# Seven steps of a window row, dealt out anew: where the residual, a centring and single taps stand in four in-order queues

## The chip, the cores and the metric

The kernel runs on one core of one Trainium2 chip. The metric is device time of one execution in microseconds (us). Engines: PE is TensorE (matrix products; PEld its weight loads), DVE is VectorE, ACT is ScalarE, POOL is GpSimd, SP issues the DMAs. Each engine takes its instructions in order, and the engines wait for one another by semaphores.

## The reference

Two layers on a batch of 16 images of 128 channels and 56 x 56 pixels, float32. The change touches the first alone, a block of attention over routed windows:

```python
x = x + dwconv3x3(x)                       # position
y = ln(x.transpose(0, 2, 3, 1), ln1)       # over channels
q, kv = split(y @ qkv_w + qkv_b)           # 7 x 7 windows of 8 x 8 pixels
idx = top_k(mean(q) . mean(k), 4)          # each window picks 4 windows
att = softmax(q_pix * SCALE @ k_sel)       # 4 heads, 64 queries x 256 keys
o = att @ v_sel + dwconv5x5(v)             # the second term is "lepe"
x = x + o @ wo_w + wo_b                    # residual
x = x + gelu(ln(x, ln2) @ w1 + b1) @ w2 + b2
```

The second layer (a 3 x 3 convolution, a small state space recurrence, a group norm) follows on the result.

## The kernel before, in words

The first layer works image by image, and each image in 49 steps, one for each window. Step t has row r = t // 7 and place c = t % 7 in the row. After the 49 steps `mlp` runs the two MLP products of seven row blocks and begins the next image. All instructions of an engine are chained in program order (`_chain`), so the order in which `step` calls its helpers is the order of every engine's queue.

What every step t does, and on which engine:

- `scores` (PE, L424) into the one buffer `ps`, then `largest` (VectorE, L430, the negated maximum), `exponentials` (ACT, L436, which reads `ps` and sums), `inverse` (VectorE, L442), `weights` (GpSimd, L446, two products).
- `attend` of window t - 2 (PE, L484), `transpose_weights` of window t - 1 (PE, L468, into `ptt`), `keep_weights` (ACT, L474).
- in even places `transpose_values` (PE, L454, into `pvt`) and `keep_values` (ACT, L461), for two windows, in c = 6 for one.
- `convolve_on`: taps of the 5 x 5 convolution on VectorE (L521 for a row's first, L527 for the others), 25 to a row, two rows in turns. `TAPS` says how many fall to each place; the last one comes at the step's end.
- `beside`: GpSimd's share of the next image's 3 x 3 convolution (L307, L323, L325), spread over all steps; `position` (L313) is that convolution's last tap, on VectorE, in six of the steps.

What a row adds, by place, for the finished row above (`out`, `row`) and for the same row of the next image (`nxt`):

- c = 0 and 1: products L364 for k and v of `nxt` into `g0` and their copies by ACT (`keep`, L370 and L373). c = 1: `collect` (VectorE, L531), `project_out` (PE, L539, into `pvt`).
- c = 2: `residual` (VectorE, L543) reads `pvt` and adds into `xh`; `centred` (PE, L329) multiplies `xh` by the centring matrix into `g0`.
- c = 3: `squared` (ACT, L333), `variance` (PE, L337, into `pvt`). c = 4: `deviation` (ACT, L341, L342), `second` (VectorE, L547: the norm's product, which reads `g0`), then `centred` for `nxt`, into `g0` again.
- c = 5 and 6: `squared`, `variance`, `deviation` for `nxt`; `windows` (VectorE, L350, L358); the product for q (L364).

`piece` issues PE's share of these. It stands ahead of `transpose_weights`, or, where `waits` holds (c = 1, 4, 6), at the end of the step. `surround` (GpSimd, L499 and two fills) copies a row of v with its neighbours into one of three buffers `vpad`, from which the taps read.

Of the kernel before, what the change touches and what calls it, by code (L numbers as in the profile page):

```python
# [209 lines left out]
def layer0(ctx: ExitStack, tc: tile.TileContext, x, t, x1, conv):  # L210
# [70 lines left out]
    def load(b, two):  # L281
        nc.sync.dma_start(pads[b % 2][64 * two : 64 * two + 64, 1 : H + 1, 1 : W + 1], xv[b, two])
# [48 lines left out]
    def squared(n):  # L331
        sq = held["sq"] = w1.tile([P, BLK], F32, tag="sq", name=f"sq_{n}")
        nc.scalar.activation(sq, held["pc"], AF.Square)  # L333
# [5 lines left out]
    def deviation(n):  # L339
        rstd = held["rstd"] = w1.tile([P, BLK], F32, tag="rstd", name=f"rstd_{n}")  # L340
        nc.scalar.activation(rstd, held["pv"], AF.Ln, bias=eps)  # L341
        nc.scalar.activation(rstd, rstd, AF.Exp, scale=-0.5)  # L342
# [3 lines left out]
    def windows(im, i):  # L346

        n = f"{im['b']}_{i}"
        y = held["y"] = w1.tile([P, BLK], F32, tag="y1", name=f"y1_{n}")
        nc.vector.tensor_mul(  # L350
            y.rearrange("c (w r x) -> c w r x", w=WIN, r=8),
            held["pc"].rearrange(by_row, r=8, w=WIN),
            held["rstd"].rearrange(by_row, r=8, w=WIN),
        )
        if i == 0:
            im["sum"] = w2.tile([P, NW], F32, tag="ysum", name=f"ysum_{n}")
            im["kv"] = w2.tile([P, NW, WP, 2], F32, tag="kv", name=f"kv_{n}")
        nc.vector.tensor_reduce(  # L358
            im["sum"][:, WIN * i : WIN * i + WIN], y.rearrange("c (w p) -> c w p", p=WP), AX.X, ALU.add
        )  # L360
# [5 lines left out]
    def keep(im, i, s):  # L366
        src = held["pq", s].rearrange("c (w p) -> c w p", p=WP)
        if s == 0:
            q = im["q"][i] = w1.tile([P, WIN, WP], F32, tag=f"q{i}", name=f"q_{im['b']}_{i}")
            nc.scalar.activation(q, src, AF.Identity, bias=bias[:, 0:1], scale=SCALE)  # L370
        else:
            kv = im["kv"][:, WIN * i : WIN * i + WIN, :, s - 1]
            nc.scalar.activation(kv, src, AF.Identity, bias=bias[:, s : s + 1])  # L373
# [27 lines left out]
    def gather(im, w):  # L401
        sel = im["sel", w] = w6.tile([P, TOPK, WP, 2], F32, tag="sel", name=f"sel_{im['b']}_{w}")
        if w % 2 == 0:
            n = min(2, NW - w)
            _, im["at"] = nc.values_load_multi_w_load_instructions(
                im["line"][:, w : w + n, :].rearrange("o w j -> o (w j)"), engines=(mybir.EngineType.SP,),
                min_val=0, max_val=NW - 1, skip_runtime_bounds_check_because="the indices are at most 48",
            )
        vs = im["at"][TOPK * (w % 2) :]
        for j in range(TOPK):  # L410
            nc.sync.dma_start(
                sel[:, j, :, :].rearrange("c p s -> c (p s)"),
                im["kv"][:, bass.ds(vs[j], 1), :, :].rearrange("c o p s -> c (o p s)"),
            )
# [76 lines left out]
    def vpad(im, r):  # L491
        return vpads[(im["b"] * NBLK + r) % 3]

    def surround(im, r):

        v = vpad(im, r)

        def put(lines, i, rows):
            nc.gpsimd.tensor_copy(  # L499
                v[:, lines, 2 : W + 2].rearrange("c r (w x) -> c w r x", x=8),  # L500
                im["kv"][:, WIN * i : WIN * i + WIN, :, 1].rearrange("c w (r x) -> c w r x", x=8)[:, :, rows, :],
            )

        put(slice(2, 10), r, slice(0, 8))
        if r == 0:
            nc.gpsimd.memset(v[:, 0:2, :], 0.0)
        else:
            put(slice(0, 2), r - 1, slice(6, 8))
        if r == NBLK - 1:
            nc.gpsimd.memset(v[:, 10:12, :], 0.0)  # L510
        else:
            put(slice(10, 12), r + 1, slice(0, 2))

    def convolve(im, r, k):

        v = vpad(im, r)
        acc = sums_[(im["b"] * NBLK + r) % 2][:, 0:BLK].rearrange("c (h w) -> c h w", w=W)
        dy, dx = divmod(k, 5)
        src = v[:, dy : dy + 8, dx : dx + W]
        if k == 0:  # L520
            nc.vector.tensor_scalar(acc, src, lep[:, 0:1], lepe_b, ALU.mult, ALU.add)  # L521
            return
        out = acc
        if k == 24:
            lepe = im["lepe", r] = w2.tile([P, BLK], F32, tag="lepe", name=f"lepe_{im['b']}_{r}")
            out = lepe.rearrange("c (h w) -> c h w", w=W)
        nc.vector.scalar_tensor_tensor(out, src, lep[:, k : k + 1], acc, ALU.mult, ALU.add)  # L527

    def collect(im, r):
        o = held["o"] = w1.tile([P, BLK], F32, tag="o", name=f"o_{im['b']}_{r}")  # L530
        nc.vector.tensor_add(  # L531
            o.rearrange("c (r w x) -> c r w x", r=8, w=WIN),
            po[:, 0:BLK].rearrange("c (w r x) -> c r w x", w=WIN, r=8),
            im["lepe", r].rearrange("c (r w x) -> c r w x", r=8, w=WIN),
        )
# [5 lines left out]
    def residual(im, r):  # L541
        xh = im["xh"][r]
        nc.vector.scalar_tensor_tensor(xh, held["pw"], wo_b, xh, ALU.add, ALU.add)  # L543

    def second(im, r):
        y2 = im["y2"][r] = w1.tile([P, BLK], F32, tag=f"y2{r}", name=f"y2_{im['b']}_{r}")
        nc.vector.tensor_mul(y2, held["pc"], held["rstd"])  # L547
# [19 lines left out]

    TAPS = (4, 2, 2, 3, 3, 3, 2)  # L570

    slot = [0]

    def convolve_on(count):


        for at in range(slot[0], slot[0] + count):
            r = at // 25
            r -= (r - at) % 2
            if 0 <= r < NB * NBLK:  # L580
                convolve(images[r // NBLK], r % NBLK, (at - 25 * r) // 2)
        slot[0] += count
# [14 lines left out]
    def open_step(im, t):  # L597
        scores(im, t)
        largest(im, t)

    def step(im, nxt, t):
        r, c = divmod(t, WIN)
        b = im["b"]
        n = f"{b}_{t}"
        out, row = (im, r - 1) if r else (images[b - 1], NBLK - 1)
        old, new = r > 0 or b > 0, nxt is not None
        if t + AHEAD < NW:
            gather(im, t + AHEAD)
        if t == 0 and early and not new:
            conv.load(0)  # L610
        if t in (20, 24) and b + 2 < NB:
            load(b + 2, t // 4 - 5)

        if c < 3 and new and r:
            keep(nxt, r - 1, c)
        if c == 2 and old:
            residual(out, row)
        if c == 3 and old:
            squared(n)
        if c == 4 and old:  # L620
            deviation(n)
        if c == 5 and new:
            squared(n)
        if c == 6 and new:
            deviation(n)
        if t > 0 or b == 0:
            open_step(im, t)
        if t > 1:
            attend(im, t - 2)
        if c == 1 and r:  # L630
            collect(im, r - 1)
        if c == 4 and old:
            second(out, row)
        if c == 6 and new:
            windows(nxt, r)
        convolve_on(TAPS[c] - 1)
        if new:
            ends, lead = (ENDS[1], LEAD) if b else (ENDS[0], FIRST)
            if t in ends:
                position(nxt, 1 + ends.index(t), (8,))  # L640
            if t < 45:
                beside_to(b + 1, lead + -(-(ROUND - lead) * (t + 1) // 45))
            else:
                beside_to(b + 2, 3 * (t - 44) // 2)
        exponentials(im, t)
        inverse(im, t)
        if t in (1, 8, 17, 27):
            surround(im, 3 + (1, 8, 17, 27).index(t))
        if t in (36, 44) and new:
            surround(nxt, (t - 36) // 8)  # L650
        weights(im, t)
        if c == 1 and new and r:
            project(g0, 2)
        waits = c in (1, 4, 6)
        if not waits:
            piece(im, nxt, out, row, c, r)
        if t > 0:
            transpose_weights(im, t - 1)
            keep_weights(im, t - 1)
        if c % 2 == 0:  # L660
            transpose_values(im, t)
            keep_values(im, t)
        convolve_on(1)
        if waits:
            piece(im, nxt, out, row, c, r)
# [85 lines left out]
    im = images[0]  # L751
# [63 lines left out]
    route(im)  # L815
    for w in range(AHEAD):
        gather(im, w)
    convolve_on(13)
    conv.bring()
    if NB > 1:  # L820
        beside_to(1, FIRST)
# [1 line left out]
    for b in range(NB):  # L823
        im, nxt = images[b], images[b + 1] if b + 1 < NB else None
# [5 lines left out]
    r = NBLK - 1  # L830
# [571 lines left out]
```

## Time and profile before

| | us |
|---|---|
| median of 3 runs | 8286.96 (8285.49 to 8291.58) |
| the profiled execution, its own time | 8287.32 |
| its span, first to last instruction | 8285.5 |
| first maximum of image 1, of image 2 | 285.9, 474.8 |
| last store's addition of the first layer ends | 3146.1 |
| first exponential of the second layer | 3187.7 |

So the first layer takes some 189 us an image. The granted TensorE clock is 0.985 of full speed over the span. In the profile a line names engine, source line, operation, the tile written and the tiles read; `sst` are the statistics of a step, `e` its exponentials, `g` is `g0`.

### The profile page before, as it was taken

Reading aid. Unit: us, or ns where it says so; the run is one execution under the profiler, and the core shown is the slowest. Engines: PE = TensorE matmul, PEld = TensorE weight load, DVE = VectorE, ACT = ScalarE, POOL = GpSimd, SP = SyncE. Lnnn points to the kernel's source line nnn. Section 1 sums busy time; section 2 is a strip of 40 time slices with the busy share of each in tenths; the row PEclk is TensorE's granted clock in tenths of the full one; section 3 lists DMA queues with packets and bytes.
Section 4 is the critical chain, followed back from the end, with each engine's and each line's share of the span. In section 5 each row is a group of like instructions: output and inputs, shape, how many; then the busy total and the mean of one; then the engine's idle time right before and its main releaser. Section 6 shows DMA issues by size and latency. Waiting matters only on the chain.

```text
span 8285.5 us, 151813 instructions
## 1 busy us (share of the span) xinstructions
PE 7838.8 (95%) x53380; PEld 3344.5 (40%) x53380; DVE 7607.8 (92%) x10105; ACT 5689.0 (69%) x10695; POOL 7010.1 (85%) x5569
## 2 busy tenths in 40 slices
PE   8999999999999998999999999999999999999998
PEld 4444444444444453333333333333333333333333
DVE  7998999999999976999999999999999999999998
ACT  5777777777777765666666666766666666666665
POOL 6888888888888725898989989999989989989897
PEclk9999999999999998999999999999999999999998
DMA  4333333333333223334333333334334344334333
GB/s 78 88 86 79 88 88 87 88 86 89 91 87 87 73 81 82 86 93 104 101 90 99 98 93 102 95 94 107 84 102 105 86 103 103 89 96 108 88 91 87
DMA packets 765510, 757.89 MB, mean 91 GB/s; under 512 B 189648, under 2 KB 664912, under 8 KB 762832
## 3 DMA queue, kind: packets, MB, share of 16 engines
q1 hardware_dynamic: 764752, 748.19, 35.4%
q8 instruction: 426, 6.98, 0.4%
q14 instruction: 332, 2.72, 0.1%
HBM read 439.61 MB, written 102.76 MB: 65 GB/s over the span
## 4 chain that ended last, share of the span: by engine, by line
PE 42%; DVE 28%; POOL 12%; ACT 10%; issue 7%; DMA 0%; SPq 0%; POOLq 0%; ACTq 0%; DVEq 0%
PE pq L185 9%; PE a L1028 9%; DVE h L1046 6%; DVE a L1056 5%; POOL xh L325 5%; PE pq L1074 4%; DVE lepe L527 4%; DVE h L1061 4%; PE x L1039 4%; POOL tap L323 3%; POOL e L446 3%; PE pq L1108 3%; DVE sst L430 2%; ACT e L436 2%; ACT a L1031 2%
## 5 line engine op out<-in xcount | busy, mean ns | idle before, releaser
L1065 POOL TENSOR_TENSOR cst<-h,cb 128x1792 f32<-128x1792 f32 x784 | 3129.1, 3998 | 337.4 <-DVE h L1061 278.1
L1031 ACT ACTIVATE a<-a 128x896 f32<-128x896 f32 x1568 | 1415.8, 903 | 1185.7 <-PE x L1039 962.8
L1046 DVE TENSOR_TENSOR h<-x,bb 128x896 f32<-128x896 f32 x1568 | 1695.6, 1081 | 131.1 <-PE x L1039 98.9
L527 DVE SCALAR_TENSOR_TENSOR lepe<-vpad,lep,lepe 128x448 f32<-128x448 f32 x2688 | 1716.8, 677 | 0.5
L1028 PE MATMUL a<-dt,adec 32*128 32x448 f32 x6272 | 1616.6, 591 | 55.7 <-DVE h L1061 53.9
L1039 PE MATMUL x<-dtx,amask 32*128 32x448 f32 x6272 | 1620.5, 593 | 40.2 <-DVE h L1046 31.1
L1056 DVE TENSOR_TENSOR a<-a,h 128x896 f32<-128x896 f32 x1344 | 1464.8, 1090 | 68.9 <-ACT a L1031 65.7
L1061 DVE TENSOR_TENSOR h<-a,h 128x896 f32<-128x896 f32 x1344 | 1465.1, 1090 | 42.0
L446 POOL TENSOR_SCALAR e<-e,sst,zero 128x256 f32<-128x256 f32 x1568 | 855.0, 555 | 573.5 <-DVE sst L442 514.2
L436 ACT ACTIVATE e<-ps,sst 128x256 f32<-128x256 f32 x1568 | 726.9, 468 | 538.1 <-DVE sst L430 493.1
L1028 PEld LDWEIGHTS a<-dt,adec 32*128 32x128 f32 x6272 | 472.6, 184 | 1060.1 <-issue 298.7
L325 POOL TENSOR_TENSOR xh<-xh,tap 128x448 f32<-128x448 f32 x742 | 849.7, 1145 | 32.9
L185 PE MATMUL pq<-pad,conv 128*128 128x448 f32 x1890 | 834.7, 559 | 0.0
L1074 PE MATMUL pq<-cst,sel 128*32 128x448 f32 x6272 | 729.9, 550 | 0.0
L430 DVE TENSOR_REDUCE sst<-ps 128x2 f32<-128x512 f32 x784 | 539.8, 688 | 111.1 <-PE ps L424 83.1
L146 ACT ACT_TABLE_LOAD x484 | 621.0, 1283 | 9.3 <-PEq L1393 0.7
L1039 PEld LDWEIGHTS x<-dtx,amask 32*128 32x128 f32 x6272 | 473.5, 184 | 319.0 <-DVE h L1046 295.2
L468 PE MATMUL ptt<-ident,e 128*128 128x128 f32 x3136 | 521.9, 281 | 71.0 <-POOL e L446 61.6
L424 PE MATMUL ps<-sel,q 32*64 32x256 f32 x6272 | 541.7, 414 | 48.3 <-ACT e L436 35.8
L468 PEld LDWEIGHTS ptt<-ident,e 128*128 128x128 f32 x3136 | 371.2, 142 | 371.3 <-issue 184.4
L474 ACT COPY att<-ptt 128x512 f32<-128x512 f32 x784 | 457.8, 584 | 62.7 <-PE ptt L468 52.9
L185 PEld LDWEIGHTS pq<-pad,conv 128*128 128x128 f32 x1890 | 324.2, 189 | 357.9 <-issue 350.2
(184 smaller groups left out, 12330.0 us busy)
## 6 DMA issues: line engine op xcount, KB each, us to landing
sel<-kv SPq DMA_DIRECT2D x3136, 64.0 KB
bb<-db SPq DMA_DIRECT2D x336, 448.0 KB
cb<-dc SPq DMA_DIRECT2D x336, 448.0 KB
x<-r SPq DMA_DIRECT2D x112, 224.0 KB
pad<-x SPq DMA_DIRECT2D x16, 1568.0 KB
db<-bs SPq DMA_DIRECT2D x112, 224.0 KB
dc<-cs SPq DMA_DIRECT2D x112, 224.0 KB
bb<-db SPq DMA_DIRECT2D x112, 224.0 KB
```

The costliest lines, as they stand in the source:

```text
L185: self.nc.tensor.matmul(bank[:, 0:BLK], lhsT=self.weights[:, k, :], rhs=self.pad[:, 8 * i + dy : 8 * i + dy + 8, dx : dx + W], start=(k == ...
L325: nc.gpsimd.tensor_add(im["xh"][i], im["xh"][i], held["tap"])
L446: nc.gpsimd.tensor_scalar(e, e, im["st", w][:, 2, p : p + 1], zero, ALU.mult, ALU.add)
L527: nc.vector.scalar_tensor_tensor(out, src, lep[:, k : k + 1], acc, ALU.mult, ALU.add)
L1028: nc.tensor.matmul(a[:, k, :], lhsT=adec[rows, l4, :], rhs=p["dt"][rows, h, :], start=True, stop=True)
L1031: nc.scalar.activation(p["a", l, jp], p["a", l, jp], AF.Exp)
L1039: nc.tensor.matmul(x[:, k, :], lhsT=mask[rows, l4, :], rhs=p["dtx"][rows, h, :], start=True, stop=True)
L1046: nc.vector.tensor_mul(p["h", l][:, own(jp), :], px["x"], weight)
L1056: nc.vector.tensor_mul(a, a, before)
L1061: nc.vector.tensor_add(h, p["a", l, jp], h)
L1065: nc.gpsimd.tensor_mul(c, p["h", l], p["gate", 1, l].unsqueeze(1).to_broadcast([P, 4, BLK]))
L1074: nc.tensor.matmul(py[32 * j : 32 * j + 32], lhsT=sel[:, l4, :], rhs=p["c", l][:, j, :], start=False, stop=(l % 4 == 3), skip_group_check= ...
```

## The change

- `residual` goes from ahead of `largest` to behind it (c = 2).
- `piece` of c = 2, which is `centred` of the finished row, goes behind both transposes, to the end of the step.
- One tap is taken out of the group and put between `windows` and `second`: in c = 4 it runs ahead of `second`.
- `TAPS` has one tap fewer in c = 0 and one more in c = 1. The sum, 19 to a row, is the same. Ahead of the first step 14 taps run instead of 13.
- GpSimd's copies move: in the image's own steps from t = 1, 8, 17, 27 to 3, 10, 17, 26, for the next image from 36 and 44 to 38 and 45.

```diff
-    TAPS = (4, 2, 2, 3, 3, 3, 2)
+    TAPS = (3, 3, 2, 3, 3, 3, 2)
...
         if c < 3 and new and r:
             keep(nxt, r - 1, c)
-        if c == 2 and old:
-            residual(out, row)
         if c == 3 and old:
             squared(n)
...
         if c == 1 and r:
             collect(im, r - 1)
+        if c == 2 and old:
+            residual(out, row)
+        if c == 6 and new:
+            windows(nxt, r)
+        convolve_on(1)
         if c == 4 and old:
             second(out, row)
-        if c == 6 and new:
-            windows(nxt, r)
-        convolve_on(TAPS[c] - 1)
+        convolve_on(TAPS[c] - 2)
...
-        if t in (1, 8, 17, 27):
-            surround(im, 3 + (1, 8, 17, 27).index(t))
-        if t in (36, 44) and new:
-            surround(nxt, (t - 36) // 8)
+        if t in (3, 10, 17, 26):
+            surround(im, 3 + (3, 10, 17, 26).index(t))
+        if t in (38, 45) and new:
+            surround(nxt, (t - 38) // 7)
...
-        waits = c in (1, 4, 6)
+        waits = c in (1, 2, 4, 6)
...
-    convolve_on(13)
+    convolve_on(14)
```

## The prediction

> **What bounds the kernel now.** The first layer ends near 3146 us (its last store's addition, L565, by the timeline); nothing behind it changes, so only its 784 steps count. Read first the page's engine line, then the busy times of the stretch 300 to 2900 us, which holds steps of the first layer alone (the numbers after the engines: clock, DMA share, GB/s).
>
> ```profile
> PE 7838.8 (95%) x53380; PEld 3344.5 (40%) x53380; DVE 7607.8 (92%) x10105; ACT 5689.0 (69%) x10695; POOL 7010.1 (85%) x5569
> ```
>
> ```profile
> 300.00:2900.00 2600.00, 2393.70 (x23241) 1275.11 (x23234) 2366.32 (x4513) 1900.05 (x5014) 2128.80 (x3080) 0.99 0.34 86
> ```
>
> In that stretch PE is busy 2394 and DVE 2366 of 2600 us: neither alone is the bound, and only the order of one row's seven steps tells which wait ends last. So next the timeline of VectorE in image 6, steps 21 to 26 (row 3; c is the step's place in the row). Columns: start, us, instruction, count, [idle before, releaser].
>
> ```profile
> 1303.26 0.68 DVE L543 SCALAR_TENSOR_TENSOR xh<-pvt,vec,xh 128x448 f32<-128x448 f32 x1
> 1303.97 0.69 DVE L430 TENSOR_REDUCE sst<-ps 128x2 f32<-128x512 f32 x1
> ...
> 1305.74 0.17 DVE L442 RECIPROCAL sst<-sst 128x2 f32<-128x2 f32 x1 [0.49 <-ACT e L436]
> ...
> 1306.80 0.69 DVE L430 TENSOR_REDUCE sst<-ps 128x2 f32<-128x512 f32 x1 [0.30 <-PE ps L424]
> ...
> 1309.45 0.69 DVE L430 TENSOR_REDUCE sst<-ps 128x2 f32<-128x512 f32 x1
> 1310.56 0.62 DVE L547 TENSOR_TENSOR y<-g,rstd 128x448 f32<-128x448 f32 x1 [0.42 <-ACT rstd L342]
> ```
>
> The maxima (L430) of c = 0 to 5 start at 1297.67, 1300.71, 1303.97, 1306.80, 1309.45 and 1313.00. VectorE stands still mainly at the two places that the change attacks: 0.49 before the reciprocal of c = 2 and 0.42 before the norm's product (L547) of c = 4. TensorE in the same steps:
>
> ```profile
> 1301.01 1.02 PE L364 MATMUL g<-y,wqkv 128*128 128x448 f32 x2 [0.28 <-ACT kv L373]
> ...
> 1303.15 0.68 PE L424 MATMUL ps<-sel,q 32*64 32x256 f32 x8
> ...
> 1305.42 0.64 PE L454 MATMUL pvt<-ident,sel 128*128 128x128 f32 x4
> 1305.98 0.68 PE L424 MATMUL ps<-sel,q 32*64 32x256 f32 x8
> ...
> 1311.23 1.02 PE L329 MATMUL g<-xh,centre 128*128 128x448 f32 x2 [0.31 <-DVE y L547]
> 1312.18 0.68 PE L424 MATMUL ps<-sel,q 32*64 32x256 f32 x8
> ```
>
> The scores (L424) end 0.13 to 0.14 before the next maximum in c = 2, 3, 4 and 5 (1303.83 to 1303.97 is the first): those maxima wait for TensorE, not for VectorE. And TensorE's queue is in order: whatever stands in front of the scores delays them. Last, step 1 of image 6 and its window (the first number behind the five engines is the granted clock):
>
> ```profile
> 1235.53 0.97 PE L468 MATMUL ptt<-ident,e 128*128 128x128 f32 x4 [1.98 <-POOL e L446]
> ```
>
> ```profile
> 1235.30:1238.40 3.10, 2.77 (x26) 1.18 (x30) 3.10 (x8) 1.50 (x5) 3.10 (x7) 0.84 0.29 85
> ```
>
> **Unit times,** start to start within a busy queue, from these rows: tap 0.595, maximum 0.60, collect 0.53, residual 0.60, norm's product 0.54, reciprocal 0.08; on PE scores 0.61 (0.68 to the end), attend 0.36, weights' transposes 0.44, values' transposes 0.57, a 448-wide product 0.85, or 0.95 where it had to wait (1311.23 to 1312.18). From a maximum's start its reciprocal can start after 1.79 (0.69, 0.04 to ACT, 1.02 for two exponentials, 0.04), the next scores after 1.80, the next maximum after 2.61: c = 5 already runs at this floor.
>
> **The residual behind the maximum, centring last in step 2.** Before, the residual (1303.26) began 0.03 after project_out ended and was done 0.03 before scores(2) allowed the maximum: it cost nothing. That maximum is reached from c = 0 by ACT and PE: exponentials, copies, keep of kv (ends 1300.96), L364 at 1301.01, transposes, project_out, scores(2) at 1303.15. None of these is touched, so largest(2) stays at 6.30 behind largest(0). After, the residual runs 0.60 to 1.28 behind largest(2). The values' transposes write pvt, whose product the residual is still reading (one buffer, L541-543), so they start after it; the row shows such a wait in L329 behind L547, which reuses g0. Then centring, then scores(3): 1.28 + 0.05 + 0.57 + 0.90 + 0.68 + 0.13 = 3.61 from maximum to maximum, against 2.83: +0.78 a row. The two uncertain links are the release (0.04 to 0.15 in rows like 1311.23 and the old residual) and the product (0.85 to 0.95): +0.72 to +0.93. VectorE saves its 0.49 before the reciprocal (residual and tap cover the 1.79) and pays more before the next maximum. Queued behind the waiting transposes are centring and scores(3), behind these the whole next step; no DMA is moved. Squared and variance now come without their 0.22 wait: c = 3 goes from 2.64 to its floor, -0.03.
>
> **The tap ahead of the norm's product (c = 4).** Before: rstd let L547 begin 1.11 behind the maximum. With variance earlier rstd is ready about 0.82 behind it, but the tap puts L547 at 0.60 + 0.595 = 1.19. Centring of the next image waits for it (it reuses g0), and scores(5) for that: 1.19 + 0.62 + 0.06 + 0.95 + 0.68 + 0.13 = 3.63 against 3.55: +0.08. VectorE's 0.42 moves behind the last tap. In step 46, where a position tap in c = 3 had hidden rstd's wait, the step was 3.16: +0.47 there.
>
> **Taps dealt anew.** One fewer in c = 0: VectorE's 3.03 falls to 2.5, but scores(1) end 2.70 behind largest(0) and the maximum comes at 2.83. That 0.20 is lost again in c = 1, because largest(2) is fixed at 6.30. Only where a position tap makes c = 1 bind (3.56, steps 15 and 36) is it kept: -0.29 and -0.17. The 14th tap ahead costs 0.6 once, and no more than that even if nothing hides it.
>
> **GpSimd's copies.** A surround is 0.65 + 2 x 0.31 at most (1.26 of groups L499, 1.04 overlapped). In c = 3 weights are needed only behind L547's centring, with some 0.4 to spare, and GpSimd idles 0.5 to 1.7 there: taken at 0 (if the cover goes, up to 0.17 in step 11). Freed steps 8, 27, 36, 44 gain nothing, as they run like their neighbours. In step 26 (3.67) position (L313, 1.30 against 0.68) waits for GpSimd's sum; c = 4's reciprocal, now 1.19 + 0.54 + 0.595 = 2.32 behind its maximum, stands 1.31 ahead of the next one instead of 0.66, and that sum runs behind its weights: -0.6, of which the surround ahead of weights(26) takes back 0.1: -0.5. In steps 0 to 2, weights(0) come a tap earlier, 1.98 of PE idle falls to about 1.4, and step 1 loses its surround. Images 1 to 14 take 11.13 there on average; image 10, at clock 1.0, took 9.52. By the sum above (3.70, 6.80, 10.4 in image 6) the mean is about 10.45: -0.7.
>
> The Trainium skill (TensorE: Matmul & The Clock Gate, What's actually happening) lets the clock halve after an idle window of about 3.4 us. The trace shows 0.84 and less after a gap of 1.98 us, and a dip in ten of the eleven images with 1.8 us or more there, so the row decides; by the page alone those dips would not be the gap's doing, and steps 0 to 2 would gain about 0.1 instead of 0.7, some 9 us less over the layer.
>
> **Sum.** Rows of an ordinary image: row 0 -0.7 + 0.1 = -0.6; row 1 0.78 - 0.03 + 0.08 = +0.83; row 2 -0.29 + 0.73 - 0.03 + 0.08 = +0.49; row 3 0.83 - 0.5 = +0.33; row 4 +0.78 (a little back in c = 6); row 5 -0.17 + 0.74 - 0.03 + 0.08 = +0.62; row 6 0.78 + 0.47 = +1.25. Together +3.70; fourteen images +52; image 0 without row 0's gain +4; image 15, without a next image's centring behind L547, loses 0.3 in c = 2 and gains 0.5 in c = 4, -1 in all (its c = 2 takes 3.29 already, held by ACT's L194, and its c = 4, 3.49, waits for VectorE alone); the lead tap +0.6. +56 us on the profiled run's own time of 8287.32 (its span 8285.5 and 1.8 around it), which stands 0.4 above the median 8286.96: **8343**.
>
> **Rivals.** (1) Faster: VectorE is the true bound and both its idles vanish, 0.91 a row x 105 rows = -95: 8192. For it: VectorE's 91% in the stretch. Against: the maxima of c = 2 to 5 start 0.13 behind the scores. It decides if largest(3) comes under 2.83 behind largest(2), that is if neither the values' transposes nor centring stand behind the residual. Chance 0.10. The Trainium skill (Perfetto Trace Analysis, Optimization Strategy) speaks for it: find the gaps of the busiest engine and make what they wait for come sooner; by that rule alone the sum would be this rival's. (2) No change: the transposes do not wait for the residual, only centring does. L2 to L3 is then 1.28 + 0.10 + 0.90 + 0.81 = 3.1, +0.27 instead of +0.78; 0.51 x 105 = 54 less: 8289. Against: pvt is one buffer. 0.08. (3) Slower still: the new PE waits, about 0.6 in c = 2 and 0.7 in c = 4, bring the half clock as 1.98 did; a dip costs about 1.2 (steps 27 at clock 0.65 took 4.32 against 3.03), and at one in every second row that is 56 x 1.2 = +67 more: 8410. Against: single gaps of 1.04 in step 27 dipped in 2 of 14 images. 0.10. The forecast itself has 0.72, with 8312 to 8374 from its links (0.1 x 105 either way) and the unsure 0.7 of row 0.
>
> **Range and chances.** 8283 to 8392 takes in the forecast, rival 2 and the near part of 3, and leaves out rival 1. About 0.2%, 17 us, can be told from no change: faster 0.10, same 0.09, slower 0.81.
>
> **What would show it.** Right: after the change the values' transposes of c = 2 show an idle of about 0.5 released by L543; c = 2 takes 3.6, c = 4 3.6, c = 0 2.83, c = 0 and 1 together still 6.3; the idles before L442 in c = 2 and before L547 are gone and stand before L430 of c = 3 (about 1.0) and c = 5 (about 0.5); step 26 is near 3.05 and the clock in steps 1 and 2 near 1. Wrong: largest(2) earlier than 6.2 behind largest(0), or c = 2 under 3.1, or dips of the clock in ordinary rows.

## The result and the profile after

The changed kernel takes 8349.51 us (median of 6 runs, 8338.45 to 8353.99) against 8291.19 us for the kernel before on the same chip (6 runs, 8285.49 to 8297.29): ratio 1.0066, 95% interval 1.0056 to 1.0076. It is slower by some 55 us by the ratio (46 to 63 by its interval) and by 58 between the medians, where +56 was forecast.

The profiled execution took 8353.17 us (span 8351.4, clock 0.987). From the first maximum of image 0 to the last of image 15 it needs 3053.6 us against 3003.3: +50.3, the "step sum" of what follows. The second layer, whose code is the same, took 13.6 us longer in this one profile (5153.0 against 5139.5); over all the traces of this study it ranges from 5136 to 5153. The four kernels with the late residual have 5145 to 5153, the others 5136 to 5145; with one trace of each, it is not settled whether that is scatter or an effect of the change. Causes are read here from the steps alone.

The stretch 300 to 2900 us (us, then the busy times of PE, PEld, DVE, ACT and POOL, clock, DMA share, GB/s):

```profile
300.00:2900.00 2600.00, 2378.91 (x22778) 1235.18 (x22777) 2293.53 (x4429) 1872.72 (x4916) 2095.35 (x3034) 1.00 0.34 85
```

VectorE is busy 73 us less in this stretch than before, and 4429 of its instructions fit in where 4513 did. The kernel is not bound by how much VectorE does. VectorE's timeline in image 6, row 3 (start, us, instruction, count, [idle before, releaser]); the first row is the maximum of c = 2:

```profile
1325.99 0.69 DVE L430 TENSOR_REDUCE sst<-ps 128x2 f32<-128x512 f32 x1 [0.41 <-PE ps L424]
1326.60 0.67 DVE L543 SCALAR_TENSOR_TENSOR xh<-pvt,vec,xh 128x448 f32<-128x448 f32 x1
...
1327.78 0.15 DVE L442 RECIPROCAL sst<-sst 128x2 f32<-128x2 f32 x1
...
1329.57 0.69 DVE L430 TENSOR_REDUCE sst<-ps 128x2 f32<-128x512 f32 x1 [1.05 <-PE ps L424]
...
1332.19 0.69 DVE L430 TENSOR_REDUCE sst<-ps 128x2 f32<-128x512 f32 x1
1332.80 0.74 DVE L521 TENSOR_SCALAR lepe<-vpad,lep,vec 128x448 f32<-128x448 f32 x1
1333.44 0.61 DVE L547 TENSOR_TENSOR y<-g,rstd 128x448 f32<-128x448 f32 x1
...
1335.88 0.69 DVE L430 TENSOR_REDUCE sst<-ps 128x2 f32<-128x512 f32 x1 [0.57 <-PE ps L424]
```

The reciprocal (1327.78) and the norm's product (1333.44) now start without a wait: both idles that the change attacks are gone. VectorE stands before the maxima instead, and for longer: 0.41 before that of c = 2, where the residual used to run, 1.05 before c = 3 (0.30 before the change), 0.57 before c = 5, all released by the scores (L424). TensorE in the same steps tells why the scores are late:

```profile
1327.33 0.74 PE L454 MATMUL pvt<-ident,sel 128*128 128x128 f32 x4 [0.53 <-DVE xh L543]
1327.91 0.92 PE L329 MATMUL g<-xh,centre 128*128 128x448 f32 x2
1328.76 0.68 PE L424 MATMUL ps<-sel,q 32*64 32x256 f32 x8
...
1334.11 1.02 PE L329 MATMUL g<-xh,centre 128*128 128x448 f32 x2 [0.43 <-DVE y L547]
1335.06 0.68 PE L424 MATMUL ps<-sel,q 32*64 32x256 f32 x8
```

The values' transposes (L454) stand 0.53 until the residual has read `pvt`; centring, the scores and the next maximum follow in one unbroken chain, 3.58 from maximum to maximum instead of 2.83. At 1334.11 centring waits 0.43 for the product that reads `g0`, 0.31 before. Medians by step over images 2 to 13:

| step | before | after | forecast |
|---|---|---|---|
| c = 0, c = 1 | 3.03, 3.26 | 2.83, 3.46 | 2.83, 3.46 |
| c = 2 | 2.83 | 3.58 | 3.61 |
| c = 3 | 2.64 | 2.61 | 2.61 |
| c = 4, step 46 | 3.55, 3.16 | 3.63, 3.62 | 3.63, 3.63 |
| step 26 | 3.67 | 3.04 | 3.05 |
| step 27 | 3.03 | 3.56 | about 3.13 |
| step 13 | 3.59 | 3.24 | 3.59 |

Step 1 of image 6, which had 1.98 of idle and the clock at 0.84:

```profile
1256.85 0.97 PE L468 MATMUL ptt<-ident,e 128*128 128x128 f32 x4 [1.40 <-POOL e L446]
```

```profile
1256.63:1259.66 3.03, 2.60 (x30) 1.14 (x30) 3.03 (x7) 1.49 (x5) 1.79 (x4) 1.00 0.29 84
```

The wait is down to 1.40 and the clock, first number behind the five engines, is full. Over images 1 to 14 the clock fell below 0.9 in step 1 of 12 images before and of 3 after; steps 0 to 2 take 10.51 on average instead of 11.12. How much of that is the change's doing is taken up behind the experiments.

Nothing in the timelines explains step 27's +0.53 yet, nor step 13's -0.35. GpSimd's timeline does the first; 1339.16 are the weights of step 26, and behind it TensorE in step 27 of the same image:

```profile
1337.77 1.26 POOL L499 COPY vpad<-kv 128x448 f32<-128x448 f32 x2
...
1339.16 1.08 POOL L446 TENSOR_SCALAR e<-e,sst,zero 128x256 f32<-128x256 f32 x2
```

```profile
1339.76 0.98 PE L468 MATMUL ptt<-ident,e 128*128 128x128 f32 x4 [1.05 <-POOL e L446]
```

The reciprocal of step 26 is done at 1338.42 (L442, 1338.26 for 0.16), but the moved copy stands in front of the weights, which start 0.74 later. The transposes of step 27 wait 1.05 us for them. That is no longer than before (1.04, where the reciprocal itself was late behind the position tap), but then the maximum of step 27 was as late; now it came early, and the next one has to wait for the scores behind these transposes.

### The profile page after: what moved, and what is told of

It is laid out like the page before. It is cut to its first block, busy times and chain, and to the rows that moved or that the text cites. A ratio compares the mean times of both kernels' runs of the same rounds, so it can differ in the third digit from the quotient of the medians.

```text
span 8351.4 us, 151717 instructions
## 1 busy us (share of the span) xinstructions
PE 7879.2 (94%) x53380; PEld 3328.7 (40%) x53380; DVE 7577.4 (91%) x10105; ACT 5699.3 (68%) x10695; POOL 7006.0 (84%) x5569
## 4 chain that ended last, share of the span: by engine, by line
PE 49%; DVE 23%; POOL 13%; ACT 6%; issue 6%; DMA 1%; SPq 1%; DVEq 0%; POOLq 0%; ACTq 0%
PE a L1029 10%; PE pq L185 9%; PE pq L1075 5%; DVE h L1047 5%; POOL xh L325 4%; DVE a L1057 4%; PE x L1040 4%; POOL e L446 4%; DVE h L1062 3%; POOL tap L323 3%; DVE sst L430 3%; DVE lepe L527 3%; PE pq L1109 2%; PE ps L424 2%; PE pq L1081 2%
## 5 line engine op out<-in xcount | busy, mean ns | idle before, releaser
L468 PE MATMUL ptt<-ident,e 128*128 128x128 f32 x3136 | 550.4, 285 | 65.6 <-POOL e L446 51.8
L424 PE MATMUL ps<-sel,q 32*64 32x256 f32 x6272 | 537.9, 411 | 65.2 <-ACT e L436 55.0
```

## The experiments

My theory was the chain just read: the residual's place behind the maximum holds the transposes, and the wait runs down TensorE's queue. The rivals on record became questions for the runs: whether an end of VectorE's waits is worth anything by itself, and which of the other parts gives or takes what. All ratios are against the kernel before on the same chip; step sums are against its 3003.3 us.

| kernel | ratio, 95% interval | step sum |
|---|---|---|
| the change | 1.0066 [1.0056, 1.0076] | +50.3 |
| residual ahead (e1) | 1.0006 [0.9997, 1.0016] | +10.7 |
| centring early (e2) | 1.0132 [1.0115, 1.0149] | +114.9 |
| centring late alone (e3) | 0.9990 [0.9981, 1.0000] | -0.4 |
| tap ahead alone (e4) | 1.0000 [0.9991, 1.0010] | +5.3 |
| copies alone (e5) | 1.0014 [1.0005, 1.0024] | +19.2 |
| taps alone (e6) | 1.0004 [0.9994, 1.0014] | +10.3 |
| squared early (e7) | 0.9984 [0.9975, 0.9994] | -6.4 |
| product ahead of the tap (e8) | 1.0041 [1.0026, 1.0055] | +36.5 |
| positions in c = 2 (e9) | 0.9986 [0.9977, 0.9995] | -16.2 |
| e9 and squared early (e10) | 0.9982 [0.9973, 0.9991] | -14.0 |
| e10 and a tap into the MLP (e11) | 0.9981 [0.9972, 0.9990] | -11.3 |
| copy back in step 27 (e12) | 1.0058 [1.0042, 1.0073] | +43.1 |

**e1, the changed kernel with the residual back ahead of the maximum.**

```diff
+        if c == 2 and old:
+            residual(out, row)
         if c == 3 and old:
             squared(n)
...
-        if c == 2 and old:
-            residual(out, row)
```

> The changed kernel with one thing undone: the residual of c = 2 stands ahead of the maximum again; centring stays late, taps and copies as changed. Theory (the values' transposes, centring and scores(3) queue behind the residual): the 0.53 idle before the values' transposes goes, L3 comes 9.1 behind L0 instead of 9.9 (c = 0 2.83, c = 1 up by 0.13 to 3.6 because the residual now ends VectorE's longer c = 1, c = 2 2.7); 0.76 less in four rows, 0.36 in rows 2 and 5, 0.16 in row 0: 57 less over fifteen images, about +0.0 to +0.1% against the kernel before. Rival (the loss lies in the tap ahead of the norm's product or in the moved copies): it stays within 15 us of the changed kernel, +0.5% or more.

It took 8301.75 (before 8295.13): the loss is all but gone. TensorE in c = 2 (step 23 of image 6):

```profile
1313.13 0.64 PE L454 MATMUL pvt<-ident,sel 128*128 128x128 f32 x4
1313.61 0.92 PE L329 MATMUL g<-xh,centre 128*128 128x448 f32 x2
```

Neither row has a wait; c = 2 takes 2.61 to 2.71, and centring stands late here too. So one moved instruction carries most of the loss: its place is worth 39.6 us of the 50.3 in the step sum, where 57 were expected, and 0.60 of the 0.66% in the ratios.

**e2, the changed kernel with centring back ahead of the transposes.**

```diff
-        waits = c in (1, 2, 4, 6)
+        waits = c in (1, 4, 6)
```

> The changed kernel with the centring of c = 2 ahead of both transposes again; the residual stays behind the maximum. Theory: now the weights' transposes wait behind the residual too: 1.28 + 0.05 + 0.95 + 0.44 + 0.57 + 0.68 + 0.13 = 4.1 for c = 2 against 3.58, so +0.52 x 105 = +55 on the changed kernel, about +1.3% on the kernel before. Rival (it is the late centring that costs, not the residual's place): c = 2 falls back to about 2.9 and the run to within 0.1% of the kernel before.

8408.08, and c = 2 takes 4.08:

```profile
1350.68 0.99 PE L329 MATMUL g<-xh,centre 128*128 128x448 f32 x2 [1.20 <-DVE xh L543]
1351.50 0.60 PE L468 MATMUL ptt<-ident,e 128*128 128x128 f32 x4
```

With the residual late, centring first waits 1.20 instead of 0.53 for the same instruction, and the weights' transposes, which could have filled the wait, stand behind it. So late centring halves the loss; it belongs to the late residual.

**e3, the kernel before with only centring late.** The edit is that of e2, the other way round.

> The kernel before with the centring of c = 2 at the step's end and nothing else. Theory (TensorE's queue bounds c = 2 and c = 4): c = 2 stays 2.83, the 0.22 wait of the variance goes and c = 3 falls to 2.61, rstd is ready 0.3 sooner, the norm's product starts 0.83 behind its maximum instead of 1.11 and c = 4 falls from 3.55 to 3.27; 0.31 in six rows of fifteen images: 28 less, -0.34%. Rival (VectorE bounds c = 4 at 3.5, or the exponentials do): no change, within 0.1%.

A miss: 8286.68, ratio 0.9990, steps the same. I had thought that c = 4's idle before the norm's product would go. It stays at 3.55 in most rows. ScalarE in c = 2 and 3 of this kernel:

```profile
1307.41 0.58 ACT L474 COPY att<-ptt 128x512 f32<-128x512 f32 x1
1307.88 0.61 ACT L461 COPY v<-pvt 128x512 f32<-128x512 f32 x1
1308.36 0.57 ACT L333 ACTIVATE sq<-g 128x448 f32<-128x448 f32 x1
```

What holds the square (L333) is not TensorE but ScalarE's own queue: two copies stand ahead of it, whatever TensorE does first.

**e4, the kernel before with only the tap ahead of the norm's product.**

```diff
-        if c == 4 and old:
-            second(out, row)
         if c == 6 and new:
             windows(nxt, r)
-        convolve_on(TAPS[c] - 1)
+        convolve_on(1)
+        if c == 4 and old:
+            second(out, row)
+        convolve_on(TAPS[c] - 2)
```

> The kernel before with only the one tap ahead of the norm's product. Theory: the product starts 1.19 instead of 1.11 behind its maximum, centring and scores(5) follow: c = 4 3.63 instead of 3.55, and 3.6 instead of 3.16 in step 46: (6 x 0.08 + 0.47) x 15 = +14, +0.17%. Rival (VectorE's 0.42 idle there is worth its length): 0.42 x 90 = 38 less, -0.45%.

c = 4 is 3.63 (+0.08) and step 46 3.63 (+0.47), to the hundredth as expected; yet the kernel as a whole stays the same (8295.9 against 8295.13). Step 26 falls from 3.67 to 3.07, and row 0 gets 0.62 shorter on average as its clock dips in 6 of 14 images instead of 12. So the tap's 0.08 in five rows and 0.47 in one are met by step 26 and by row 0. That row 0 is the tap's doing is not shown: the wait in step 1 is the old one (1.98 in image 6, as before the change). Against them stand steps 29 and 30 with 0.8 on average, which come from a few images; e11 shows what they wait for.

**e5, the kernel before with only GpSimd's copies moved** (both step tuples as in the change).

> The kernel before with GpSimd's copies at the new steps and nothing else. Theory (copies are hidden but for one): steps 3, 10, 38, 45 do not change; step 26 stays 3.67, its weights run behind the copy and step 27 grows by 0.3 to 0.5; rows 0 to 2 lose at most 0.5; the run within 10 us of the kernel before. It also tells whether the 0.27 that VectorE stood before the maximum of step 14 (gone in the changed kernel, without a releaser in either trace) hangs on the copies: step 13 3.59 or 3.24. Rival (the copies are part of the loss): +20 us or more.

A miss: within 10 us was expected, and the ratio gives +12 (4 to 20 by its interval), the steps +19.2. Of these 18.3 lie in step 27, which goes from 3.24 to 4.38 on average over the images, where 0.3 to 0.5 was expected. TensorE there in image 6, and the window of that step:

```profile
1325.40 0.97 PE L468 MATMUL ptt<-ident,e 128*128 128x128 f32 x4 [1.67 <-POOL e L446]
```

```profile
1324.57:1329.02 4.45, 3.52 (x24) 1.42 (x28) 3.08 (x8) 2.51 (x7) 3.83 (x8) 0.75 1.00 151
```

The wait for the weights is 1.67 here, and the clock falls to 0.75 over the step: TensorE is busy 3.52 of its 4.45. So one copy of 1.26 us costs up to 2.0, where the long gap brings the slow clock as well. The other rows move by less than 0.03 in the median, except row 0, which gets 0.33 shorter on average. That is no more than in e3 and e7 (0.48 and 0.44), which leave steps 0 and 1 as they were, so it is not shown to be the copies' doing.

**e6, the kernel before with only the taps dealt anew.**

```diff
-    TAPS = (4, 2, 2, 3, 3, 3, 2)
+    TAPS = (3, 3, 2, 3, 3, 3, 2)
...
-    convolve_on(13)
+    convolve_on(14)
```

> The kernel before with the taps dealt as in the change (one fewer in c = 0, one more in c = 1, 14 ahead). Theory: c = 0 falls to 2.83 by scores(1), but with the residual ahead of the maximum the longer c = 1 now ends it: maximum 2 comes 6.43 behind maximum 0, and centring, which waits for the residual, pushes maximum 3 to 9.3 against 9.12; +0.2 in four rows, +0.5 in rows 2 and 5, -0.5 in row 0: +1.3 x 15 = +19, +0.23%. Rival (VectorE is the bound and only the number of taps counts): no change.

c = 0 is 2.83 and the way from c = 0 to c = 3 grows from 9.13 to 9.28, rows 2 and 5 by 0.46 and 0.34, much as expected (to 9.3, and 0.5). But row 1 falls by 0.25 instead of growing: step 13 is 3.24, as in the changed kernel, where it was 3.59 with a stall of 0.27 on VectorE ahead of the next maximum. In the kernel before (image 6):

```profile
1276.15 0.69 DVE L430 TENSOR_REDUCE sst<-ps 128x2 f32<-128x512 f32 x1 [0.27 <-POOL e L446]
```

The profile puts the stall down to GpSimd's weights of step 13, but by the kernel's code nothing in the maximum of step 14 reads or overwrites what they touch. Every kernel with the old `TAPS` has the stall (before, e3, e4, e5, e7, e9 to e11), every one with the new does not (the change, e1, e2, e6, e8, e12). It goes with the taps; why was not found.

**e7, the kernel before with the square right behind c = 2's exponentials.**

```diff
-        if c == 3 and old:
-            squared(n)
...
+        if c == 2 and old:
+            squared(n)
```

> The kernel before with ACT's squared of the finished row straight behind the exponentials of c = 2, ahead of the two copies, instead of at the head of c = 3. The late centring alone gave nothing because squared still stood behind those copies on ACT. Theory: squared ends 2.2 behind maximum 2 instead of 3.2, the variance no longer waits 0.22, c = 3 is 2.61, rstd is ready 0.8 behind maximum 4, the norm's product starts there and c = 4 falls to 3.27: 0.3 in six rows of fifteen images, 27 less, -0.33%. Rival (c = 4 is held by VectorE's own work or by the weights' transposes): c = 4 stays above 3.45, no change.

8282.74, ratio 0.9984: half of what was expected by the ratio, and a quarter by the steps (6.4 of 27). The square starts at once behind the exponentials, but the variance does not:

```profile
1302.47 0.54 ACT L333 ACTIVATE sq<-g 128x448 f32<-128x448 f32 x1
...
1303.36 0.61 ACT L461 COPY v<-pvt 128x512 f32<-128x512 f32 x1
```

```profile
1304.03 1.02 PE L337 MATMUL pvt<-sq,mean 128*128 128x448 f32 x2
```

It writes `pvt`, which the copy of the values (1303.36) reads until 1303.97; L337 starts 0.06 later, some 0.13 later than the products ahead of it on TensorE alone would have let it. The same buffer that makes the residual dear in the change holds back part of the gain here. c = 4 becomes 3.51; a row gains 0.07.

**e8, the changed kernel with the norm's product ahead of the tap again.**

```diff
-        convolve_on(1)
         if c == 4 and old:
             second(out, row)
-        convolve_on(TAPS[c] - 2)
+        convolve_on(TAPS[c] - 1)
```

> The changed kernel with the norm's product ahead of the tap again. Theory: rstd is ready 0.82 behind maximum 4 in the changed kernel, the tap holds the product until 1.26; without it the product starts at 0.85, c = 4 falls from 3.63 to 3.3 and from 3.62 to 3.2 in step 46; (6 x 0.34 + 0.4) x 15 = 37 less than the changed kernel, of which step 26 takes back up to 9: about +0.3% on the kernel before. Rival (c = 4 is bound elsewhere): the changed kernel's time, +0.66%.

8329.67, 1.0041. VectorE and TensorE in c = 4:

```profile
1326.90 0.62 DVE L547 TENSOR_TENSOR y<-g,rstd 128x448 f32<-128x448 f32 x1 [0.16 <-ACT rstd L342]
```

```profile
1326.90 0.64 PE L454 MATMUL pvt<-ident,sel 128*128 128x128 f32 x4
1327.58 1.02 PE L329 MATMUL g<-xh,centre 128*128 128x448 f32 x2
```

With VectorE idle for 0.16 ahead of the product, centring starts as soon as the transposes let it, and c = 4 is 3.29 instead of 3.63. Accepting the idle is worth 0.34 a row. The step sum gains 13.8, though, and not 28. That step 26 goes back to 3.66 was in the 28; what was not is mainly row 0 and step 27, where the clock falls more often than with the change: steps 0 to 2 take 10.94 instead of 10.51 (dips in step 1 of 11 images instead of 3), step 27 3.94 on average instead of 3.73.

**e9, the kernel before with the position taps where VectorE has time to spare.**

```diff
-    ENDS = ((7, 15, 23, 30, 38, 45), (1, 5, 15, 26, 36, 45))
+    ENDS = ((7, 15, 23, 30, 38, 45), (2, 9, 16, 30, 37, 45))
```

> The kernel before with the six position taps of VectorE in steps 2, 9, 16, 30, 37, 45 instead of 1, 5, 15, 26, 36, 45: five of them now in c = 2, between the maximum and the reciprocal. Theory (c = 2 is bound by TensorE's queue and VectorE has 0.8 to spare there): c = 2 stays 2.83 to 2.9, and what the old places cost goes: 0.43 in step 5, 0.3 each in steps 15 and 36, 0.9 in steps 26 and 27 with the wait for GpSimd's sum, perhaps 0.3 in step 1: 2.0 x 14 = 28 less, -0.34%. Rival (VectorE's total work bounds a row): no change, and c = 2 grows by 0.6.

The kernel is faster, 8281.3 against 8293.62. VectorE in c = 2, with the position tap L313 in it:

```profile
1320.45 0.69 DVE L430 TENSOR_REDUCE sst<-ps 128x2 f32<-128x512 f32 x1
...
1321.64 1.09 DVE L313 SCALAR_TENSOR_TENSOR xh<-y,pos,xh 128x448 f32<-128x448 f32 x1
...
1323.31 0.68 DVE L430 TENSOR_REDUCE sst<-ps 128x2 f32<-128x512 f32 x1
```

The step stays at 2.83 to 2.86 with 1.0 us more work in it: VectorE's idles were real room, to be filled and not to be closed. Steps 5, 15, 26 and 36 fall by 0.42, 0.31, 1.05 and 0.33 as expected, but steps 6, 18, 27 and 29 take some 0.8 of it back, and about 40% of the expected gain is left by the ratio, 60% by the steps.

**e10, e9 with the square early and the copy of step 1 in step 3; e11, e10 with one tap of step 0 moved into the MLP.**

```diff
-        if t in (1, 8, 17, 27):
+        if t in (3, 8, 17, 27):
...
-        convolve_on(TAPS[c] - 1)
+        convolve_on(TAPS[c] - 1 - (t == 0 and b > 0))
...
-                convolve_on((7, 7, 6, 6, 6)[m - 1])
+                convolve_on((7, 7, 6, 6, 7 if nxt else 6)[m - 1])
```

> As the run with the position taps in c = 2, with squared behind the exponentials of c = 2 and the copy of step 1 moved to step 3. Theory: the gains add, 0.07 a row from squared and 0.3 in rows 0 from the copy, 12 more: -0.5% on the kernel before. Rival: squared collides with the later reciprocal of c = 2 and gives nothing: -0.34%.

> As the run with the position taps in c = 2, squared early and the copy of step 1 moved, and in step 0 of images 1 to 15 one tap fewer, which runs in mlp before it, where VectorE idles 5 us. Theory: weights(0) come 0.6 earlier, TensorE's idle ahead of the weights' transposes falls from 1.9 to 1.3 and the clock stays up in step 1 as in the changed kernel (3 dips in 14 images against 11 or 12): steps 0 to 2 take 10.2 instead of 11.0, 12 less, -0.33% on the kernel before. Rival (the tap only moves its time into mlp): -0.18% as without it.

8277.51 and 8280.23, ratios 0.9982 and 0.9981: both are some 0.18% under the kernel before, the lowest of this study (e7 and e9 lie within their intervals), and neither comes near what was expected. In e10 rows gain 0.08 by the square as in e7, but step 1's clock dips in 11 of 14 images again and step 29 grows by 0.6 on average. In e11 steps 0 to 2 fall to 9.72, more than expected although the clock still dips in 8 of 14 images; the step that holds the MLP, where the tap went, grows by 0.7 and step 29 by 1.1. What step 29 waits for stands in the trace; TensorE at its end, in image 6 of e11:

```profile
1323.59 0.68 PE L424 MATMUL ps<-sel,q 32*64 32x256 f32 x8 [1.18 <-DMA sel<-kv]
```

The scores of step 30 wait for the transfer that gathers their keys. Over images 1 to 14 this wait comes in 4 images of e4 and of e9, 5 of e10 and 10 of e11, with 0.4, 0.4, 0.6 and 1.2 us an image, and in none of the kernel before or of the changed one. So a part of what the faster steps won was lost to a transfer that was not there yet; why it lands late just there was not tested.

**e12, the changed kernel with the copy of step 26 back in 27.**

> The changed kernel with the one copy of step 26 back in step 27. Theory (the prediction's term for step 26 failed because that copy stands ahead of weights(26)): step 27 falls from 3.56 to 3.0, step 26 stays 3.04: 0.53 x 15 = 8 less than the changed kernel, +0.56% on the kernel before. Rival: step 27 is held by something that the shorter step 26 uncovers: no change, 3.5.

8342.05, 1.0058: steps 26 and 27 take 3.04 and 3.03, and the step sum is 7.2 lower than with the change, that is 0.5 in each of fourteen images. The transposes of step 27 in image 6:

```profile
1339.33 0.97 PE L468 MATMUL ptt<-ident,e 128*128 128x128 f32 x4 [0.42 <-POOL e L446]
```

They wait 0.42, 0.63 less than with the copy in front, and 0.53 of it reaches the maximum of step 28. This settles step 27.

## Why the prediction was right

The forecast was 8343, the time 8349.51, and the loss came for the reason given: c = 2 and c = 4 were limited by what TensorE's queue waits for, not by how much VectorE does.

- **The residual.** Forecast +0.78 a row, measured +0.75; the 0.05 of release and the 0.90 for centring were 0.06 and 0.85. e1 shows that the place of this one instruction carries most of the loss, and e2 that centring's new place limits it. The maximum of c = 2 stayed 6.29 behind that of c = 0 (6.30 forecast).
- **The tap and step 46.** +0.08 and +0.46 (forecast +0.08 and +0.47); e4 has them alone. e8 shows what the step could have been: 3.29, with VectorE waiting.
- **A right sum for a part with a wrong reason.** I had the square and the variance come earlier once centring is late. e3 refutes that as a matter of order: ScalarE's copies stand in front. c = 3's 0.03 came only because the maximum of c = 3 came 0.75 later, and the square was done by then.
- **Row 0: a right size, but not by the reason given.** Forecast -0.7 for steps 0 to 2, measured -0.61, with dips in step 1 of 3 images instead of 12. The prediction had the length of the wait decide over the dip. The runs do not bear that out. e4 has the old steps 0 and 1 and the old waits, yet 6 dips and 10.39 for steps 0 to 2; e3 and e7, which also leave these two steps alone, have 9 dips each. The five kernels with the change's steps 0 and 1 (the change, e1, e2, e8, e12) have 3, 8, 6, 11 and 5. What the dips go with is how the wait falls on the clock's grid (last section), and that differs from run to run, so how much of the 0.61 the change earned stays open.
- **The mis-sized term: the copy in step 26.** The prediction took 0.1 of step 26's gain back for the surround ahead of weights(26). It costs 0.53 (e12), and 1.1 on average without the other edits (e5). The step that failed: it set the copy against GpSimd's slack before the next maximum, and did not follow the weights behind it to the transposes and the scores of the step after. Of the -0.5 of row 3, -0.1 was left.
- **What was not foreseen:** step 13's stall of 0.27 and with it 0.35 of row 1; row 1 grew 0.42, not 0.83. Row 5 grew 0.49, not 0.62. These errors are opposite in sign to that of the copy: over steps 0 to 47 of images 1 to 14 the forecast's sum was 3.70 an image and the measured one 3.66. With the step that holds the MLP it is 3.49, and the steps of all images gave 50.3 where the forecast had 55; what the time has on top lies outside the steps, where the forecast had nothing and the second layer took 13.6 longer in the trace. The closeness of the total is partly luck. The inner range of 8312 to 8374 is also wider than the two terms named for it: 0.1 x 105 and 14 x 0.7 make 20, not 31.

The rivals: VectorE as the true bound (8192) falls, since its two idles are gone and the kernel is slower. The Trainium skill (Perfetto Trace Analysis, Optimization Strategy), cited for that rival, asks to find the gaps of the engine one optimizes for and to make what they wait for come sooner. The change closed the gaps by reordering instead, and the 0.49 and 0.42 came back as 0.41, 1.05 (0.30 before) and 0.57 elsewhere; e7, which did make the awaited square come sooner, gained 0.07 a row. What no run here bears out is that such a gap is worth its length. Transposes that do not wait for the residual (8289) fall by the 0.53 released by L543. Clock dips in ordinary rows (8410) fall: the waits there are 0.4 to 0.5, and dips in images 1 to 14 begin only in steps 0, 1 and 27.

## What to carry to other kernels

An engine's idle time is worth only what stands last behind it: before closing a gap, follow the chain one step on and ask which in-order queue takes it over. When a reader of a shared PSUM buffer moves behind another instruction, its next writer moves too, and everything queued behind that writer; here one move of 0.67 us of work cost 0.75 in each row. Fill a gap that cannot be closed with work that has to be done anyway (e9), and before moving a filler, look who waits for the instruction behind it. When steps get shorter, look also whether the transfers still land in time (step 30 in e9 to e11).

## What the runs showed of the hardware

- In all fourteen traces the recorded clock is either full or half, and all its changes in a trace lie on one grid of 3.41 us, whose phase differs from run to run. A fall goes with how busy TensorE was in the last piece of that grid: between 300 and 2900 us, of the pieces at full clock in which it was busy for less than 45% (by the profile's busy times), 65 of 66 were followed by the half clock, at 45 to 55% 52 of 71, at 55 to 65% 18 of 176, and above that none of 10186. So the same wait can bring a dip or not. The wait of 1.98 in step 1 of image 6 fell with 1.53 into one piece in the kernel before (first two rows; PE is the first number behind the comma, the clock the first behind the engines), and the next piece has the half clock. In e4 an edge split it into 1.28 and 0.70 (last two rows), and the clock stayed full:

```profile
1234.00:1237.41 3.41, 1.78 (x10) 0.88 (x14) 3.41 (x9) 1.32 (x5) 2.63 (x5) 1.00 0.40 125
1237.41:1240.83 3.42, 3.42 (x29) 1.64 (x22) 2.87 (x6) 1.20 (x5) 3.42 (x7) 0.50 0.33 96
```

```profile
1229.05:1232.47 3.42, 1.99 (x15) 0.96 (x13) 2.84 (x7) 1.54 (x5) 2.54 (x3) 1.00 0.29 105
1232.47:1235.88 3.41, 2.60 (x30) 1.15 (x30) 3.41 (x7) 1.50 (x5) 3.31 (x7) 1.00 0.32 93
```

- The Trainium skill (TensorE: Matmul & The Clock Gate, What's actually happening) has the two rates and a free-running window of 3413 ns, and these traces agree. It lets the clock fall after an idle window of about 3.4 us; here a piece in which TensorE was still busy for about half of the time was often enough.
- VectorE stood 0.27 us ahead of the maximum of step 14 in images 1 to 14, in each of the eight kernels with the old deal of taps and in none of the six with the new. What stops it there is open.
- Code that is the same need not take the same time: the second layer ranged over 17 us in the fourteen traces, a third of what the change costs, and why is open. Effects of 10 us were read from the steps, not from one total.
